# Layer 2's window attention: from one tile after another to a loop of slots in fixed order

## The chip, the cores and the metric

The program runs on one core of one Trainium2 chip. Its time is the device time of one execution in microseconds (us), and lower is better. The core has five engines that work side by side and meet at semaphores: TensorE (PE; weight loads are listed as PEld), VectorE (DVE), ScalarE (ACT), GpSimd (POOL) and SyncE (SP), which here only issues transfers. All data is 32-bit float.

## What is computed

Four layers run over two images of 1024 tokens with 256 channels. Layers 0 and 1 are global attentions; layer 2 is a window attention and a mixture of experts; layer 3 is an additive attention and a second mixture of experts. The change is inside layer 2, between the end of layer 1 and the first expert. In the reference, cut to what matters (the roll by half a window is done beforehand, by the way x is loaded):

```python
# t: (2, 1024, 256); H = 8 heads of D = 32; windows of 64 tokens
u = ln(t)                                          # over the 256 channels
q, k, v = (u @ w_qkv.T + b_qkv) by head
sim = (q . k) * D ** -0.5 + rel_pos[head, i - j]   # inside each window
sim = where(mask, -inf, sim)                       # last window of an image
out = softmax(sim) @ v                             # per head, heads joined
t = t + out @ w_out.T + b_out
# experts: route every token to two of 8
probs = softmax(ln(t) @ Wr + br);  top two, weights normalised to sum 1
t = t + sum over the two of weight * (gelu(xn @ W1[e] + b1[e]) @ W2[e] + b2[e])
```

The experts' own layer norm has a gain and a bias for each expert, so a routed token is normalised twice.

## The kernel before

**Tiles.** The tokens are 16 tiles of 128 (NT = 16), 8 to an image (IT = 8), two windows to a tile. `t` holds tokens on partitions, `uT` channels on partitions in two chunks of 128 (CC = 2). `CH` is 512 tokens, four tiles.

**Norm and turn.** After layer 1, `run` turns the stream into `t` (L846 to L851). `layer_norm` then normalises all 16 tiles (statistics L100, a square root on ScalarE L89, L104), and `to_channels` turns them into `uT` (L115 to L120). The small loads of the later layers (`Late.__init__`, such as L929's input `sb_wa`) go out on SP's queue at the same time.

**Window attention.** `scores(i)` projects q and k for four tiles at a time (L734, L740, L742), then v for its tile (L752, L756; a column of ones is appended to each head by L749), takes the scores of both windows (L767), scales them and adds the relative bias (L772), subtracts the row maximum (L778, L779), and writes the exponentials, not yet normalised, into the block diagonal of a 128x128 matrix per head (L782). `values(i)` turns these eight matrices on TensorE (L790, copied out by L791 on ScalarE and VectorE), multiplies each with its head's values (L795; the ones column yields the row sums), normalises the result (L797, L799), turns it into channels (L803, L805), projects it (L808), adds the bias (L812), and adds it into `t` on GpSimd (L813). The loop emits `scores(i + 1)` ahead of `values(i)`.

**Routing.** When tile 7, the last of image 0, has been emitted, `after` runs all of `dispatch(2, 0)` at once: `norm` and `channels` for the image (L956 to L974), the router (L1040), some 60 small VectorE operations that rank the experts and give each token two slots (L1044 to L1136), with a count over the tokens on TensorE in their middle (L1072), a second norm, 16 indirect transfers that scatter the tokens to their slots in memory (L1006, on GpSimd's queue), and 8 steps that add the experts' output bias (L1015 to L1021).

**Order.** In all of layer 2 a planner in the framework sets the order on each engine: an instruction that it holds to be ready goes first by its place in the program's text, and one of later text fills a gap. So an engine may draw later work ahead. Only where a `manual_schedule` stands do the engines named in it keep the order of the text. After the attention, `Late.run` merges the rest by a plan: each entry names a generator, what must be issued ahead of it, start and end on a common scale, and a number of pieces. E20 (experts of image 0) runs from 0 to 185, D21 (routing of image 1) from 5 to 165. For an expert tile the tokens are loaded from the slots (`xr`, L1168), the two weight matrices are gathered by an indirect transfer (`ew`, L1158), and the products are L1201 and L1215.

## Time and profile before

| What | us |
|---|---|
| Median of the runs shown (3204.81 to 3214.53) | 3204.91 |
| Profiled execution | 3201.66 |
| Its span | 3200.0 |
| Norm and turn, then first projection (L734) | 1789 to 1813.5 |
| Window attention, image 0 | 1813.5 to 1911 |
| Routing of image 0 | 1911 to 1960 |
| Window attention, image 1 | 1960 to 2033 |
| First load of expert inputs (L1168) | 2033.46 |
| Experts of image 0 | to 2234 |

The profile was taken in one execution, and every instruction in it has a start and a duration on its engine. A group such as "L790 x128" is one line of the kernel with all its executions. The view of busy time by stretch sums each engine's work between two marks and gives the clock that TensorE was granted, 1.00 being full speed. The chain of work follows, back from an end, what released each step. "Idle before, releaser" is how long an engine stood before an instruction and what it stood for. An average over the whole program says little here, since the stages have different limits; the stretches from 1789 to 2234 us are the ones to read.

### The profile page before, as it was taken

Reading aid. Unit: us, or ns where it says so; the run is one execution under the profiler, and the core shown is the slowest. Engines: PE = TensorE matmul, PEld = TensorE weight load, DVE = VectorE, ACT = ScalarE, POOL = GpSimd, SP = SyncE. Lnnn points to the kernel's source line nnn. Section 1 sums busy time; section 2 is a strip of 40 time slices with the busy share of each in tenths; the row PEclk is TensorE's granted clock in tenths of the full one; section 3 lists DMA queues with packets and bytes.
Section 4 is the critical chain, followed back from the end, with each engine's and each line's share of the span. In section 5 each row is a group of like instructions: output and inputs, shape, how many; then the busy total and the mean of one; then the engine's idle time right before and its main releaser. Section 6 shows DMA issues by size and latency. Waiting matters only on the chain.

```text
span 3200.0 us, 71583 instructions
## 1 busy us (share of the span) xinstructions
PE 2927.8 (91%) x29446; PEld 1895.9 (59%) x29446; DVE 1877.1 (59%) x3723; ACT 1998.1 (62%) x2980; POOL 403.5 (13%) x558
## 2 busy tenths in 40 slices
PE   7999999999999998999999787899899898997937
PEld 4565566656666656566667454798566432663726
DVE  5998898989898987355345454543422323233333
ACT  1887788888788886466466221211588887777801
POOL 3000000000000000000000002233211202224223
PEclk9999999999999999899999786899999998998968
DMA  3000000000000000000000100488554201554526
GB/s 120 3 3 3 3 3 3 3 3 3 3 3 3 3 3 16 13 1 2 1 1 2 25 1 27 176 317 309 196 196 176 75 1 65 168 161 130 180 78 226
DMA packets 179894, 216.08 MB, mean 68 GB/s; under 512 B 118816, under 2 KB 147120, under 8 KB 167792
## 3 DMA queue, kind: packets, MB, share of 16 engines
q0 software_dynamic: 36864, 175.17, 16.0%
q1 hardware_dynamic: 141264, 35.87, 5.0%
q8 instruction: 232, 3.80, 0.5%
q14 instruction: 94, 0.77, 0.1%
q10 hardware_dynamic: 1440, 0.47, 0.1%
HBM read 181.24 MB, written 29.49 MB: 66 GB/s over the span
## 4 chain that ended last, share of the span: by engine, by line
PE 84%; DVE 4%; DMA 4%; issue 4%; POOL 2%; ACT 1%; SPq 0%; POOLq 0%; ACTq 0%; DVEq 0%
PE ps_o L358 15%; PE ps_s L282 15%; PE ps_h L1201 8%; PE ps_y L1215 7%; PE ps_e L1351 7%; PE ps_t L340 5%; PE ps_s L153 4%; PE ps_o L220 4%; PE ps_t L183 4%; PE ps_v L1388 2%; PE ps_t L642 2%; DMA slots_in<-u,rt_slot 2%; PE ps_av L795 1%; PE ps_out L537 1%; PE ps_mm L734 1%
## 5 line engine op out<-in xcount | busy, mean ns | idle before, releaser
L319 ACT ACTIVATE sc<-sc,sa_shift 128x1024 f32<-128x1024 f32 x512 | 585.1, 1148 | 51.1 <-DMA sa_shift<-sa_min 50.9
L1342 ACT ACTIVATE th<-kT,qb 128x1024 f32<-128x1024 f32 x512 | 541.4, 1134 | 99.7 <-PE ps_e L1351 90.0
L282 PE MATMUL ps_s<-kT,qT 64*32 64x512 f32 x8192 | 503.8, 596 | 9.3 <-ACT sc L292 8.7
L358 PE MATMUL ps_o<-wt,v 128*64 128x128 f32 x6144 | 503.6, 276 | 0.0
L358 PEld LDWEIGHTS ps_o<-wt,v 128*64 128x64 f32 x6144 | 442.4, 137 | 42.6 <-issue 42.6
L332 DVE STREAM_TRANSPOSE wt<-sc 128x768 f32<-128x768 f32 x512 | 465.7, 943 | 0.4 <-ACT sc L319 0.4
L292 ACT COPY sc<-ps_s 128x1024 f32<-128x1024 f32 x256 | 257.5, 1006 | 118.4 <-PE ps_s L282 43.4
L1201 PEld LDWEIGHTS ps_h<-xe,ew 128*128 128x128 f32 x2320 | 284.5, 198 | 60.2 <-issue 38.2
L1201 PE MATMUL ps_h<-xe,ew 128*128 128x128 f32 x2320 | 298.8, 284 | 14.6 <-DMA ew<-in_l_up,rt_rows 8.4
L303 DVE TENSOR_REDUCE sa_least<-sc 128x1 f32<-128x1024 f32 x256 | 306.1, 1196 | 1.6 <-ACT sc L292 1.5
L289 DVE TENSOR_SCALAR_CACHE_REDUCE sc<-ps_s 128x1024 f32<-128x1024 f32 x256 | 301.4, 1177 | 6.1 <-PE ps_s L282 6.1
L1351 PE MATMUL ps_e<-th,pick 128*32 128x512 f32 x2048 | 297.9, 621 | 3.2 <-DVE sc_a L1358 2.9
L1215 PE MATMUL ps_y<-ew,h 128*128 128x256 f32 x1160 | 274.4, 385 | 8.9 <-ACT h L1190 7.3
L159 DVE TENSOR_SCALAR_CACHE_REDUCE sc<-ps_s 128x1024 f32<-128x1024 f32 x128 | 151.8, 1222 | 179.2 <-PE ps_s L153 179.1
L1215 PEld LDWEIGHTS ps_y<-ew,h 128*128 128x128 f32 x1160 | 213.1, 191 | 68.0 <-issue 19.3
L358 PE MATMUL ps_o<-wl,v_odd 128*64 128x128 f32 x2048 | 252.3, 277 | 0.0
L282 PEld LDWEIGHTS ps_s<-kT,qT 64*32 64x32 f32 x8192 | 126.6, 106 | 200.4 <-issue 170.6
L1190 ACT ACTIVATE h<-hb 128x512 f32<-128x512 f32 x145 | 90.4, 624 | 246.0 <-DVE hb L1206 232.6
L1206 DVE TENSOR_TENSOR hb<-ps_h,ew 128x512 f32<-128x512 f32 x145 | 100.2, 691 | 236.7 <-PE ps_h L1201 210.4
L340 PEld LDWEIGHTS ps_t<-ident,sc 128*128 128x128 f32 x1024 | 107.5, 141 | 216.2 <-issue 167.8
L358 PEld LDWEIGHTS ps_o<-wl,v_odd 128*64 128x64 f32 x2048 | 221.5, 137 | 0.0
L340 PE MATMUL ps_t<-ident,sc 128*128 128x128 f32 x1024 | 168.5, 287 | 4.6 <-ACT wl L341 3.9
(272 smaller groups left out, 3579.5 us busy)
## 6 DMA issues: line engine op xcount, KB each, us to landing
xr<-slots_in SPq DMA_DIRECT2D x99, 128.0 KB, 3.2
slots_out<-y SPq DMA_DIRECT2D x99, 128.0 KB, 3.5
sa_got<-sa_least SPq DMA_DIRECT2D x512, 0.5 KB, 1.8
sa_shift<-sa_min SPq DMA_DIRECT2D x512, 0.2 KB, 1.7
slots_in<-zero POOLq DMA_DIRECT2D x46, 128.0 KB, 2.2
sa_sums<-sa_total SPq DMA_DIRECT2D x256, 1.0 KB, 1.8
xT<-in_x SPq DMA_DIRECT2D x4, 496.0 KB, 5.1
ew<-in_l_up,rt_rows POOLq DMA_INDIRECT x99, 5.7
```

The source lines that it names most:

```text
L282: nc.tensor.matmul(ps[r][S * c : S * (c + 1), a, :].rearrange("p (b i) -> p b i", i=S), lhsT=qT[half, p, S * i : S * (i + 1)], rhs=keys[ha ...
L289: nc.vector.tensor_scalar(scores[m][0], flat[0], 1.0, None, ALU.mult, ALU.min, accum_out=least[m // 2][:, 0, h : h + 1])
L292: nc.scalar.copy(scores[m][1], flat[1])
L303: nc.vector.tensor_reduce(least[m // 2][:, 1, h : h + 1], scores[m][1], AX.X, ALU.min)
L319: nc.scalar.activation(scores[m][r], scores[m][r], AF.Exp, bias=shift[m // 2][:, r : r + 1], scale=-1.0, accum_out=total[i][:, 2 * p + r, ...
L332: nc.vector.transpose(weights[i, h][:, 2 * p + r, :], scores[m][r][:, :DIRECT])
L340: nc.tensor.transpose(ps[:, g, r, :], s[:, at : at + P], self.ident)
L358: nc.tensor.matmul(sums[i][64 * k : 64 * (k + 1)], lhsT=values, rhs=w, start=(h == 0 and j == 0 and t == 0), stop=(h == 1 and j == 1 and t ...
L1201: nc.tensor.matmul(ps[:, j, :], lhsT=a[:, c, at : at + P], rhs=x[:, c, :], start=(c == 0), stop=(c == CC - 1),)
L1215: nc.tensor.matmul(ps, lhsT=h[:, j, :], rhs=w2[:, j, :], start=(j == 0), stop=(j == HB - 1))
L1342: nc.scalar.activation(h, keys, AF.Tanh, bias=self.qb[b][:, s // G, g : g + 1])
L1351: nc.tensor.matmul(pe[i][c * U : (c + 1) * U, a, :], lhsT=self.pick[:, k, :], rhs=h[:, a, :], start=(k == 0), stop=(k == G - 1),)
```

## The change

The attention becomes a loop of 20 slots whose order on TensorE and ScalarE is that of the text. A tile passes through five stages in five slots: value and scores in slot i, turn in i + 2, sums in i + 3, output in i + 4. The projections are taken in quarters, four slots ahead. The weights are normalised before they are turned: VectorE takes the row sum and its reciprocal, and GpSimd multiplies the exponentials by it while it writes them into the block diagonal (a ring of three). Both halves of the turned weights are copied by ScalarE. The sums have the values as TensorE's stationary operand and the turned weights as the moving one, so that the result has channels on partitions, and the second turn goes. The ones column goes too.

The norm and the turn are done for each image: image 0 ahead of the loop, image 1 in slots 0 to 5. They use `Late.norm`, whose inverse root is computed with VectorE operations alone. The routing of image 0 enters the loop from slot 10, three steps to a slot, and what is left of it goes into the plan as D20. The functions `layer_norm` and `to_channels` are removed.

```diff
@@ -684,7 +656,10 @@
-    def window_attention(self, t, u, uT, after):
+    def window_attention(self, t, late):
+
+
+
         tc, nc = self.tc, self.nc
@@ -694,6 +669,7 @@
             sb = ctx.enter_context(tc.tile_pool(name="wa_sb", bufs=2))
             psum = lambda name, bufs: ctx.enter_context(tc.tile_pool(name=name, bufs=bufs, space=PSUM))
             p_mm, p_s, p_av = psum("wa_mm", 3), psum("wa_s", 1), psum("wa_av", 1)
+            late.misc = lambda shape, name: p_mm.tile(shape, F32, name=name, tag="ps_mm")
             w_qkv = self.load(w, "w_qkv", "(c p) o -> p c o", p=P)
             w_out = self.load(w, "wa_w_out", "(c p) o -> p c o", p=P)
@@ -719,45 +695,47 @@
             nc.vector.memset(last[WIN + SHIFT : P, :, 0:SHIFT], MASKED)
-            probs = [w.tile([P, H, P], F32, name=f"probs{i}") for i in range(2)]
...
+            RING = 3
+            probs = [w.tile([P, H, P], F32, name=f"probs{i}") for i in range(RING)]
+            for x in probs:
+                nc.gpsimd.memset(x, 0.0)
+
+            uT, q, k, v, pT, o = {}, {}, {}, {}, {}, {}
+
+            def normed(b):
+
+                u = w.tile([P, IT, C], F32, name="u")
+                uT[b] = w.tile([P, CC, N], F32, name=f"uT{b}")
+                yield from late.norm(lambda i: u[:, i, :], lambda i: t[:, b * IT + i, :], range(IT))
+                for half in range(2):
                     for c in range(CC):
...
-                v[i] = sb.tile([P, H, D + 1], F32, name="va", bufs=3)
-                nc.gpsimd.memset(v[i][:, :, D : D + 1], 1.0)
...
+                        ps = late.misc([P, 4, P], "ps_tr")
+                        for j in range(4):
+                            nc.tensor.transpose(ps[:, j, :], u[:, 4 * half + j, c * P : (c + 1) * P], self.ident)
+                        to = uT[b][:, c, half * CH : (half + 1) * CH].rearrange("p (k t) -> p k t", t=P)
+                        (nc.scalar.copy if c else nc.vector.tensor_copy)(to, ps)
+                        yield
+
+            def project(g, part):
+
+                if part == 0:
+                    q[g], k[g] = (sb.tile([P, CC, CH], F32, name=n) for n in ("qh", "kh"))
+                x, at = uT[g // 2], g % 2 * CH
+                ps = late.misc([P, CH], "ps_qk")
                 for c in range(CC):
                     nc.tensor.matmul(
...
+                        ps, lhsT=w_qkv[:, c, part * P : (part + 1) * P], rhs=x[:, c, at : at + CH],
                         start=(c == 0), stop=(c == CC - 1),
                     )
...
+                to = (q if part < CC else k)[g][:, part % CC, :]
+                if part < CC:
+                    nc.scalar.activation(to, ps, AF.Identity, bias=b_qk[:, part : part + 1])
+                else:
+                    nc.vector.tensor_scalar(to, ps, b_qk[:, part : part + 1], None, ALU.add)
+
+            def scores(i):
+
+                g, at = i // 4, (i % 4) * P
                 s = p_s.tile([P, 4, CH], F32, name="ps_s")
                 for o in range(CC):
                     for h in range(4):
@@ -768,56 +746,94 @@
                                 s[WIN * r : WIN * (r + 1), h, WIN * o : WIN * (o + 1)],
                                 lhsT=q[g][rows, o, cols], rhs=k[g][rows, o, cols], start=True, stop=True,
                             )
...
+                l = sb.tile([P, H, WIN], F32, name="l", bufs=3)
                 nc.vector.scalar_tensor_tensor(
                     l.rearrange("p (h o) k -> p h (o k)", o=CC), s[:, :, : CC * WIN], float(D) ** -0.5,
...
+                    (last if (i + 1) % IT == 0 else bias).rearrange("p (h o) k -> p h (o k)", o=CC),
                     ALU.mult, ALU.add,
                 )
...
+                m, rec = (self.small.tile([P, H], F32, name=f"wa_{n}") for n in ("m", "rec"))
                 nc.vector.tensor_reduce(m, l, AX.X, ALU.max)
                 nc.vector.tensor_tensor(l, l, broadcast(m, [P, H, WIN]), ALU.subtract)
+                nc.scalar.activation(l, l, AF.Exp)
+                nc.vector.tensor_reduce(m, l, AX.X, ALU.add)
+                nc.vector.reciprocal(rec, m)
                 for r in range(2):
                     rows = slice(WIN * r, WIN * (r + 1))
-                    nc.scalar.activation(probs[i % 2][rows, :, rows], l[rows], AF.Exp)
...
-                    nc.tensor.matmul(av[:, of, :], lhsT=ptT[:, h, :], rhs=v[i][:, of, :], start=True, stop=True)
...
+                    nc.gpsimd.tensor_tensor(
+                        probs[i % RING][rows, :, rows], l[rows], broadcast(rec[rows], [WIN, H, WIN]), ALU.mult
+                    )
+
+            def value(i):
+                x = uT[i // IT][:, :, i % IT * P : (i % IT + 1) * P]
+                v[i] = sb.tile([P, C], F32, name="va", bufs=4)
+                ps = late.misc([P, C], "ps_va")
                 for c in range(CC):
                     nc.tensor.matmul(
...
+                        ps, lhsT=x[:, c, :], rhs=w_qkv[:, c, 2 * C :], start=(c == 0), stop=(c == CC - 1)
+                    )
+                nc.vector.tensor_tensor(v[i], ps, b_v, ALU.add)
+
+            def turn(i):
+                pT[i] = sb.tile([P, H, P], F32, name="ptT")
+                for half in range(2):
+                    ps = late.misc([P, H // 2, P], "ps_pt")
+                    for h in range(H // 2):
+                        nc.tensor.transpose(ps[:, h, :], probs[i % RING][:, H // 2 * half + h, :], self.ident)
+                    nc.scalar.copy(pT[i][:, H // 2 * half : H // 2 * (half + 1)], ps)
+
+            def sums(i):
+
+                ps, x, y = p_av.tile([P, CC, P], F32, name="ps_av"), pT.pop(i), v.pop(i)
+                for o in range(CC):
+                    for h in range(4):
+                        at = D * (4 * o + h)
+                        nc.tensor.matmul(
+                            ps[D * h : D * (h + 1), o, :], lhsT=y[:, at : at + D], rhs=x[:, CC * h + o, :],
+                            start=True, stop=True,
+                        )
+                to_o(i, ps)
+
+            def to_o(i, ps):
+                o[i] = sb.tile([P, CC, P], F32, name="oT")
+                nc.scalar.copy(o[i], ps)
+
+            def output(i):
+                x = o.pop(i)
+                ps = late.misc([P, C], "ps_wo")
+                for c in range(CC):
+                    nc.tensor.matmul(
+                        ps, lhsT=x[:, c, :], rhs=w_out[:, c, :], start=(c == 0), stop=(c == CC - 1)
                     )
                 y = sb.tile([P, C], F32, name="y")
                 nc.vector.tensor_tensor(y, ps, b_out, ALU.add)
                 nc.gpsimd.tensor_tensor(t[:, i, :], t[:, i, :], y, ALU.add)
-            scores(0)
...
-                values(i)
...
+            for _ in normed(0):
+                pass
+            route, other = late.dispatch(2, 0), normed(1)
+            engines = mybir.EngineType
+            with tc.manual_schedule(engines={engines.PE, engines.Activation}):
+                for part in range(2 * CC):
+                    project(0, part)
+                for i in range(NT + 4):
+                    if i < NT:
+                        value(i)
+                        scores(i)
+                    if 2 <= i < NT + 2:
+                        turn(i - 2)
+                    if i + 4 < NT:
+                        project(i // 4 + 1, i % 4)
+                    if i < 6:
+                        next(other, None)
+                    if 3 <= i < NT + 3:
+                        sums(i - 3)
+                    if 4 <= i:
+                        output(i - 4)
+                    if i >= 10:
+                        for _ in range(3):
+                            next(route, None)
+            return route
@@ -851,21 +867,7 @@
                             nc.vector.tensor_copy(to, ps)
             late = Late(ctx, self, t)
...
-                self.layer_norm(u, t, 1e-5)
...
-                    self.to_channels(uT, u, psum)
...
-            late.run()
+            late.run(self.window_attention(t, late))
 class Late:
@@ -1412,7 +1414,7 @@
-    def run(self):
+    def run(self, route):
         psum = lambda name, bufs: self.ctx.enter_context(self.tc.tile_pool(name=name, bufs=bufs, space=PSUM))
         p_m = psum("lt_m", 2)
         self.sb = self.ctx.enter_context(self.tc.tile_pool(name="late_sb", bufs=2))
@@ -1420,7 +1422,8 @@
         self.p_x, self.p_h, self.p_y, self.p_e = psum("lt_x", 1), psum("lt_h", 2), psum("lt_y", 1), psum("lt_e", 1)
         plan = {
-            "E20": (self.experts(2, 0), (), 0, 185, 72),
+            "D20": (route, (), -12, 0, 24),
+            "E20": (self.experts(2, 0), ("D20",), 0, 185, 72),
             "D21": (self.dispatch(2, 1), (), 5, 165, 48),
             "C20": (self.collect(2, 0), ("E20",), 186, 225, 20),
             "E21": (self.experts(2, 1), ("D21",), 186, 440, 72),
@@ -1439,7 +1442,7 @@
         }
         self.issued = set()
         at = {name: start for name, (_, _, start, _, _) in plan.items()}
-        now = 0
+        now = min(at.values())
         def merge(until):
             nonlocal now
```

## The prediction

> **What bounds the kernel now.** First the whole chain of work that ended last: TensorE holds 84% of it, so time is won only where that chain holds something else, or TensorE work that can go. Then the busy time by stretch, cut at the marks of layer 2: norms (1789 to 1813 us), window attention of image 0 (to 1911), its routing (to 1960), attention of image 1 (to 2033), the start of the experts, the experts of image 0.
>
> ```profile
> PE 84%; DVE 4%; DMA 4%; issue 4%; POOL 2%; ACT 1%; SPq 0%; POOLq 0%; ACTq 0%; DVEq 0%
> ...
> 1813.00:1911.00 98.00, 82.49 (x668) 58.25 (x669) 48.85 (x117) 25.39 (x43) 6.35 (x15) 0.85 0.00 1
> 1911.00:1960.00 49.00, 25.08 (x117) 16.30 (x116) 30.96 (x141) 0.91 (x3) 7.66 (x8) 0.53 0.05 17
> 1960.00:2033.00 73.00, 60.70 (x415) 46.53 (x415) 33.39 (x92) 16.57 (x30) 15.11 (x23) 0.85 0.05 19
> 2033.00:2040.00 7.00, 3.54 (x15) 2.10 (x13) 5.72 (x22) 0.00 (x0) 5.23 (x6) 0.50 0.74 256
> 2040.00:2234.00 194.00, 191.77 (x1284) 176.73 (x1284) 82.20 (x236) 34.27 (x52) 60.74 (x63) 0.98 0.87 319
> ```
>
> Columns: stretch, length, busy PE, PE weight loads, DVE, ACT, POOL, granted clock, DMA share, GB/s. The experts fill TensorE at clock 0.98; the attention takes 98/8 = 12.3 us a tile with no engine full, and the routing takes 49 us with TensorE half busy at clock 0.53. Next, the chain through one tile, in order of time:
>
> ```profile
> 1977.98 0.45 PE ps_pt L790 x4
> 1978.43 0.03 ACTq L791
> 1978.46 0.04 issue
> 1978.50 0.59 ACT ptT L791
> 1979.09 0.14 issue
> 1979.23 1.96 PE ps_av L795 x16
> 1981.18 0.02 issue
> 1981.21 0.22 DVE wa_rec L797
> 1981.43 0.02 issue
> 1981.45 0.44 DVE o L799
> 1981.89 0.14 issue
> 1982.02 0.42 PE ps_mm L803 x2
> ```
>
> Weights are turned, copied, summed, normalised, turned again and projected, each waiting for the last: a chain of latencies inside a tile. Last, GpSimd's order of time, with the scatter of tokens to expert slots:
>
> ```profile
> 1951.00 0.97 POOL L1006 DMA_INDIRECT slots_in<-u,rt_slot  x1 [1.70 <-DMA slots_in<-u,rt_slot]
> 1953.68 0.97 POOL L1006 DMA_INDIRECT slots_in<-u,rt_slot  x1 [1.72 <-DMA slots_in<-u,rt_slot]
> ```
>
> Each of the 16 scatters waits until the one before has landed: 2.67 us each, 42.7 us in a row. They start at 1942.3 and the last is issued at 1990.9; now the second image's attention hides them.
>
> **The slot, part by part** (warm durations from the timeline). TensorE: value 4 matmuls, 0.86; scores 32 in 0.49 (L767); turn 8 in 1.04 (L790); one quarter of a projection, 6.87/4 = 1.72 (L734, slots 0 to 11); output 0.9. *Removed:* 16 sums with 128-column weights, 1.96, and the turn of o, 0.42, with the waits between. *Added:* 16 sums with 32-column weights and 128 moving columns; no row has this form. The nearest is layer 1's L220 (64 columns, 128 moving), 32 in 1.97, so 16 take 1.0. The Trainium skill ("TensorE: Matmul & The Clock Gate", LDWEIGHTS) prices a load at its columns over 1.2 ns: 27 ns, 16 in 0.43. I take 1.0; the bounds move a slot by 0.6, 16 slots by 9 us. Sum: 0.86 + 0.49 + 1.04 + 1.72 + 1.0 + 0.9 = **6.0 us**, without projection 4.3.
>
> ScalarE: one Exp of 128x512 in place of two of 64x512 (0.63 each), two copies at 0.585 (one was DVE's), oT 0.37, half a q at 0.69: 2.5. Its fixed order puts exp(i) ahead of the copies of turn(i-2); exp(i) starts 0.6 + 3 x 0.7 = 2.7 after scores(i) (as 1902.97 to 1906.30 shows with one copy between), so the copies end some 5.4 into the slot. Bank reuse then holds output to about 5: hidden under the 6.0 with projection; without it a slot is 4.8.
>
> DVE: value 0.42, scale and bias 0.69, max 0.69, subtract 0.68, sum 0.69, reciprocal 0.21, y 0.42, half a k at 0.75: 4.2, below 6.0.
>
> GpSimd: two multiplies of 64x512 and the add into t. The row is L813, 128x256 in 0.728, DVE's like add L812 0.425. Twice the elements per partition: at most 1.46, so 2 x 1.46 + 0.73 = 3.65. The skill ("GPSIMD Engine Reference", Engine selection) speaks against this: two-input elementwise work is about twice as slow there, and the section 1 table has its port contended by DVE instructions with two SBUF inputs. Its 2.6 cycles an element at 1.2 GHz give 1.11 each, 2.95 a slot. Beside DVE's subtract, L813 once took 1.11 instead of 0.73 (1879.29): all stretched so, 5.5. All three stay below 6.0, and the turn comes two slots later, so row and rule give the same slot; I take 3.65. Queued behind a multiply are the adds into t and the scatters; the memset of the ones column (L749), on which the queue now stands for TensorE, is gone. SP's queue has nothing behind the expert input loads that is due earlier.
>
> **The sum, in profile time.** Norm of one image only: half of 16 normalisations (0.33 apart) and of the 8.9 us of turns saves 2.7 + 4.4, less a little: projections start at 1807, not 1813.5. The sqrt on ScalarE becomes 12 small DVE operations of 0.2, covered by DVE's wait for the sb_wa load until 1802.6, which stays. Without the cover, 2.4 us. First projections 8.9: **1816**. Slots 0 to 3: two of 3.1, then 6.5 each, since turn(0) waits for the Exp table (1.28) and the new chain sum, reciprocal, multiplies: 19, **1835**. Slots 4 and 5 with the other image's turns, 7.2 each; 6 to 9 at 6.0: **1873.5**.
>
> Routing of image 0 enters as three steps a slot from slot 10. All it issues counts. Slot 10, turns, 7.4. Slot 11 ends in a stall: output(7), y 0.42, GpSimd add up to 1.4, statistics 0.6, inverse root 2.4, four normalisations 1.4, with DVE queueing some 7 us with TensorE standing, since its order is fixed: 13.5. Slot 12, 4.8 and the router's 32 matmuls (4.4 warm, L1040): 9.2. Slot 13 waits for 15 DVE operations of 0.26 amid the slot's own: 9. **1912.5**. From the counts to the first scatter it is now 5 us with DVE free; here DVE also owes 4.2 a slot and 9.7 for the second norm: 12. First scatter **1925**. Attention itself ends near 1939 (two slots of 6, a drain of 13).
>
> So the end of the stage moves to the scatters. The D20 leftovers (7 scatters, 8 bias steps at 1.92 each, L1019) go to the late plan; the bias steps (15 us) hide beside the scatters and the scatters do not. 16 x 2.67 = 42.7 bare; now 48.6 from first to last issue with other POOL work between, plus 2.4 to land. I take 48: the first expert input is loaded at **1973**, now 2033.46: **60.5 saved**. Expert weights can be fetched meanwhile, but up to six 1 MB loads slow scatters: image 1's, under such load, are 81 us from first to last.
>
> **The experts of image 0** (2033 to 2234): 23 tiles at 7.24 (spacing of the input loads), TensorE-full. In it stand 13.5 us of image 1's routing: turns 1.0, router 4.4, counts 0.7, bias 8 x 0.9. With TensorE idle from 1939 to 1973 the planner may draw these ahead: 0 to 13.5; I take 9, and 3 for weights that are there already (first up-matmul now 6.5 after the load). **12**. All later work keeps its order.
>
> Sum: 60.5 + 12 = 72.5; span 3200.0 to 3127.5, the profiled time 3201.66 to 3129.2. The median of the runs, 3204.91, lies 3.2 above the profiled one: **3132 us**.
>
> **Rivals.** (a) *Scatters earlier, gap filled:* sums at 0.43, no stall at slot 11 because the planner draws norms ahead (it did: L956 of tile 0 at 1841.8), first scatter 1912, all 13.5 drawn ahead: 3132 - 13 - 5 = 3114. For: DVE gaps. Against: DVE owes about 61 us in slots 10 to 16. (b) *Fixed order stretches the slots:* TensorE stands for DVE or GpSimd at 8 us a slot in place of 6 (28 us over 14 slots): 3160. For: in-order ScalarE with exp ahead of copies. (c) *Slower:* GpSimd becomes the bound, if half-height multiplies with a broadcast cost far more than their row. It decides from slots of 6 + 72.5/14 = 11.2 us, where 2m + 0.73 = 11.2, m = 5.2 us a multiply. At 6 us, 12.7 a slot: 3132 + 14 x 6.7 = 3226. Against: L813. (d) *Nothing won:* experts start no sooner because scatters crawl beside weight loads at 5.1 us each from the first: 1925 + 82 = 2007, still 26 saved: 3166 with the 12.
>
> **Chances.** Likeliest 0.58, (a) 0.17, (b) 0.13, (d) 0.05, (c) 0.05, no change 0.02. A difference under 0.3% (10 us) is what a measurement of this kernel can't tell from none. Range 3106 to 3162: (a) with a few us of better luck, up to (b); outside it (c), (d) and the tail. Faster 0.93, same 0.02, slower 0.05.
>
> **What would show it.** Right: slots 6 to 9 near 6 us with TensorE full; GpSimd's multiplies 1.1 to 1.5; no L797, L799, L803; a stall before image 0's second turns; the first xr load just behind the sixteenth scatter with attention over 30 us earlier; image 1's router ahead of the first up-matmul. Wrong: scores or turns waiting for GpSimd, weight loads between scatters stretching them to 5 us, or an xr load that does not wait for scatters.

## The result, and the profile after

The changed kernel takes 3158.78 us (median; 3157.64 to 3160.96) against 3204.86 for the kernel before, a ratio of 0.9849 with a 95% interval of 0.9836 to 0.9863. The forecast was 3132 us with a range of 3106 to 3162. So the sign and the range held, and the size did not: the profiled span went from 3200.0 to 3156.0, 44.0 us, where the sum said 72.5.

The chain of work that ended last, by engine, in the changed kernel:

```profile
PE 83%; DVE 6%; issue 3%; DMA 3%; POOL 2%; ACT 1%; SPq 0%; another core or an unknown queue 0%; POOLq 0%; ACTq 0%; DVEq 0%
```

VectorE has gone from 4% to 6% of it, the transfers from 4% to 3%. Busy time by stretch (columns as before), cut at the marks of the changed kernel: norm, slots 0 to 5, slots 6 to 9, slot 10 to the end of the attention, two stretches up to the first expert, experts of image 0.

```profile
1790.00:1814.00 24.00, 14.29 (x56) 8.71 (x57) 21.02 (x92) 5.43 (x12) 3.11 (x11) 0.79 0.35 79
1814.00:1851.00 37.00, 31.07 (x344) 18.66 (x343) 26.12 (x45) 11.83 (x23) 12.07 (x12) 0.95 0.01 1
1851.00:1882.00 31.00, 25.12 (x274) 15.80 (x273) 23.98 (x62) 8.00 (x18) 10.28 (x12) 0.94 0.00 1
1882.00:1956.00 74.00, 53.25 (x529) 37.33 (x527) 59.60 (x200) 15.42 (x34) 28.18 (x30) 0.82 0.03 10
1956.00:1994.00 38.00, 20.50 (x75) 12.48 (x75) 28.98 (x138) 0.26 (x1) 15.08 (x17) 0.57 0.55 194
1994.00:2007.00 13.00, 10.14 (x24) 4.41 (x25) 6.00 (x24) 0.00 (x0) 7.16 (x8) 0.50 0.37 121
2007.00:2184.00 177.00, 176.66 (x1220) 165.60 (x1220) 59.50 (x123) 31.44 (x49) 54.15 (x58) 0.99 0.91 317
```

In slots 6 to 9 VectorE (third pair) is almost as busy as TensorE, and from slot 10 to 1994 us it is the busiest engine. Two stretches, 51 us, still run at a clock of 0.50 to 0.57 before the experts fill TensorE. A good part of the missing gain lies there.

**The slots.** The value matmul (L772) opens a slot. Slots 6 to 9 take 6.6, 7.5, 7.7 and 9.1 us, not 6.0. The chain of waits there, in order of time:

```profile
1857.80 1.03 POOL probs L763
...
1860.03 0.74 POOL t L810
1860.79 0.44 DVE n_st L958
...
1861.44 0.59 DVE l L750
1862.05 0.70 DVE wa_m L756
1862.77 0.70 DVE l L757
1863.51 0.04 issue
1863.56 0.64 ACT l L758
1864.22 0.70 DVE wa_m L759
...
1865.31 1.04 POOL probs L763
```

TensorE isn't in it. The planner has drawn the statistics of image 0's routing norm (L958) ahead, one tile to a slot, as VectorE isn't one of the engines in fixed order. L958 of tile i-4 waits for the add into `t` on GpSimd (L810), which is queued behind the two multiplies of slot i (L763); those wait for slot i's softmax on VectorE; and the softmax of slot i+1 (L750 onwards) is queued behind L958. The circle closes at 7.51 us (1857.80 to 1865.31).

**The scatters.** GpSimd's order of time, last column the idle time and what ended it:

```profile
1980.35 0.99 POOL L1008 DMA_INDIRECT slots_in<-u,rt_slot  x1 [3.31 <-DMA slots_in<-u,rt_slot]
1983.95 0.97 POOL L1008 DMA_INDIRECT slots_in<-u,rt_slot  x1 [2.61 <-DMA slots_in<-u,rt_slot]
1992.39 1.03 POOL L1008 DMA_INDIRECT slots_in<-u,rt_slot  x1 [7.47 <-DVE rt_lg L1103]
1993.73 0.97 POOL L1008 DMA_INDIRECT slots_in<-u,rt_slot  x1 [0.30 <-issue]
```

Image 0's scatters start at 1937.45 and the first expert input is loaded at 2002.12, 64.7 us later. Six weight loads stand among them (from 1955.26 to 1980.35 the scatters are 4.2 us apart in the mean, in the kernel before 2.67), and the scatter at 1992.39 is image 1's first one: it waits 7.47 us for its own routing while image 0's last three stand behind it. This looked like the loss. It was not the only one, as the next view says: TensorE just ahead of the experts.

```profile
1994.39 0.37 PE L1017 MATMUL ps_wT<-ident,rt_p 128*8 128x128 f32 x1 [7.11 <-DVE rt_p L1134]
1995.65 1.22 PE L1021 MATMUL ps_b<-sb_l_b,wT 8*128 8x256 f32 x2 [0.89 <-DVE wT L1019]
...
2004.65 0.63 PE L1178 MATMUL ps_x<-ident,xr 128*128 128x128 f32 x2
2005.25 1.22 PE L1021 MATMUL ps_b<-sb_l_b,wT 8*128 8x256 f32 x2
2006.40 0.38 PE L1017 MATMUL ps_wT<-ident,rt_p 128*8 128x128 f32 x1
2006.57 1.06 PE L1203 MATMUL ps_h<-xe,ew 128*128 128x128 f32 x4
```

The first up-matmul (L1203) follows without a gap on the bias steps (L1017, L1021) of *image 1*, which begin when image 1's routing has run through VectorE. The expert input is turned (L1178) 1.9 us before. In e8 below, where no bias step stands between that turn and L1203, L1203 starts 3.4 us after the load; by that, an estimate, it could have started here at 2005.6. So the input and the bias steps come due within about 1 us of each other: as long as the bias steps stay ahead of L1203, an earlier input alone wins nothing.

### The profile page after: what moved, and what is told of

The parts are those of the page before. It is cut to its first block, busy times and chain, and to the rows that moved or that the text cites. A ratio compares the mean times of both kernels' runs of the same rounds, so it can differ in the third digit from the quotient of the medians.

```text
span 3156.0 us, 71520 instructions
## 1 busy us (share of the span) xinstructions
PE 2890.6 (92%) x29414; PEld 1853.4 (59%) x29414; DVE 1882.7 (60%) x3729; ACT 1988.0 (63%) x2975; POOL 435.6 (14%) x575
## 3 DMA queue, kind: packets, MB, share of 16 engines
q0 software_dynamic: 36864, 175.17, 16.5%
## 4 chain that ended last, share of the span: by engine, by line
PE 83%; DVE 6%; issue 3%; DMA 3%; POOL 2%; ACT 1%; SPq 0%; another core or an unknown queue 0%; POOLq 0%; ACTq 0%; DVEq 0%
PE ps_o L330 15%; PE ps_s L254 15%; PE ps_h L1203 8%; PE ps_y L1217 8%; PE ps_e L1353 7%; PE ps_t L312 5%; PE ps_s L125 4%; PE ps_o L192 4%; PE ps_t L155 4%; PE ps_v L1390 2%; PE ps_t L614 2%; DMA slots_in<-u,rt_slot 1%; PE ps_out L509 1%; PE ps_qk L443 1%; POOL got L1263 1%
## 5 line engine op out<-in xcount | busy, mean ns | idle before, releaser
L1203 PEld LDWEIGHTS ps_h<-xe,ew 128*128 128x128 f32 x2320 | 281.9, 196 | 52.5 <-issue 30.4
L1203 PE MATMUL ps_h<-xe,ew 128*128 128x128 f32 x2320 | 295.3, 282 | 7.2 <-DVE xe L1182 3.8
L341 POOL TENSOR_TENSOR diag<-ident,sa_rec 32x128 f32<-32x128 f32 x64 | 24.9, 389 | 1171.9 <-DVE sa_rec L338 1171.9
```

The source lines that it names most:

```text
L1203: nc.tensor.matmul(ps[:, j, :], lhsT=a[:, c, at : at + P], rhs=x[:, c, :], start=(c == 0), stop=(c == CC - 1),)
```

## The experiments

Runs are compared by the time since the first value matmul of the same execution, because the layers before reach it between 1811.5 and 1816.9 us in these runs. "Attention ends" is the start of the last add into `t`; "first up" is L1203, "first gather" the end of image 0's experts.

| Kernel | median us | ratio to before [95%] | slot 10 | first scatter | attention ends | first up | first gather |
|---|---|---|---|---|---|---|---|
| changed kernel | 3158.78 | 0.9849 [0.9836, 0.9863] | 68.2 | 123.1 | 142.0 | 192.3 | 369.5 |
| e1_add_vector | 3151.77 | 0.9832 [0.9811, 0.9852] | 63.3 | 119.7 | 133.2 | 188.7 | 365.8 |
| e2_hold_stats | 3152.25 | 0.9833 [0.9816, 0.9849] | 60.4 | 119.8 | 138.7 | 189.3 | 367.5 |
| e3_scatter_order | 3156.40 | 0.9852 [0.9832, 0.9872] | 66.9 | 123.0 | 141.8 | 192.4 | 370.8 |
| e4_scatter_weights | 3155.81 | 0.9847 [0.9823, 0.9871] | 67.0 | 123.1 | 141.9 | 181.8 | 370.0 |
| e5_experts_first | 3152.46 | 0.9831 [0.9805, 0.9858] | 66.9 | 123.0 | 143.9 | 182.6 | 367.2 |
| e6_all | 3140.36 | 0.9802 [0.9776, 0.9828] | 63.3 | 119.7 | 132.7 | 175.3 | 360.0 |
| e7_vector_multiply | 3151.11 | 0.9832 [0.9807, 0.9857] | 63.9 | 121.4 | 138.7 | 187.8 | 366.2 |
| e8_planner_order | 3146.49 | 0.9817 [0.9793, 0.9842] | 63.6 | 122.9 | 130.1 | 187.5 | 367.1 |
| e9_route_after | 3172.07 | 0.9905 [0.9888, 0.9921] | 68.2 | 141.4 | 118.8 | 206.8 | 383.2 |
| e10_planner_all | 3131.71 | 0.9777 [0.9761, 0.9794] | 56.5 | 109.6 | 116.9 | 163.0 | 348.8 |
| e11_vector_all | 3147.10 | 0.9824 [0.9807, 0.9840] | 63.9 | 121.6 | 138.7 | 178.0 | 362.2 |
| e12_bias_scalar | 3135.41 | 0.9776 [0.9761, 0.9792] | 57.1 | 112.0 | 119.5 | 164.7 | 350.4 |

All intervals but those of e6, e9, e10 and e12 overlap that of the changed kernel, so the marks inside the executions carry the reading, not the medians. The marks have a spread too, since each is read from one execution: up to slot 10 e3, e4 and e5 do the same work as the changed kernel and reach it at 66.9 to 67.0 us, the changed kernel at 68.2. The difference lies in slots 2 and 3, which no edit touched.

### Does the circle set the slots? (e1, e2)

First way to open it: the add off GpSimd's queue.

```diff
-                nc.gpsimd.tensor_tensor(t[:, i, :], t[:, i, :], y, ALU.add)
+                nc.vector.tensor_tensor(t[:, i, :], t[:, i, :], y, ALU.add)
```

> The add of the attention's output into t (L810) on VectorE instead of GpSimd; nothing else is edited. Theory A (closed loop): slots 6 to 9 take 7.7 us because the statistics L958 of the routing norm, drawn ahead between two slots on VectorE, wait for the add into t on GpSimd, which stands behind the slot's two multiplies L763. On VectorE the add no longer stands behind them: slots 6 to 9 fall to 6.0 to 6.5 us (the value matmul L772 of slot 10 starts near 1877 in place of 1882.5), the first scatter L1008 comes near 1930 in place of 1937.45, and the time is 3149 to 3154 us (after: 3158.8). Rival B (VectorE itself is slowed while GpSimd multiplies, or has too much to do): VectorE gets 0.42 us a slot more, the slots stay at 7.7 to 8.1 us and the time is 3158 to 3166 us.

Second way: leave the add, and hold the statistics. `issue_after(x)` queues the instructions that its block emits for x's engine behind x; it sets an order only.

```diff
-                nc.vector.reciprocal(rec, m)
+                made = nc.vector.reciprocal(rec, m)
+                if i == 9:
+                    late.hold = made.ins
...
-        for k, i in enumerate(tiles):
-            nc.vector.bn_stats(st[:, k, :], src(i))
-            nc.vector.bn_aggr(mv[:, k, :], st[:, k, :])
+        with self.tc.issue_after(self.hold) if self.hold else ExitStack():
+            for k, i in enumerate(tiles):
+                nc.vector.bn_stats(st[:, k, :], src(i))
+                nc.vector.bn_aggr(mv[:, k, :], st[:, k, :])
```

> The statistics L958/L959 of image 0's routing norm are queued on VectorE behind the reciprocal L760 of slot 9; the add into t stays on GpSimd. Theory A (closed loop): slots 6 to 9 fall from 7.7 to about 6.1 us, as in slots before the statistics are drawn ahead; the statistics of four tiles (4 x 0.6 us) then stand in slot 10, which grows by up to 2.4 us. Net 3 to 5 us: time 3153 to 3156 us. Rival B (GpSimd's multiplies slow VectorE, whatever stands on it): slots 6 to 9 stay above 7.3 us, slot 10 grows, time 3159 to 3163 us.

In e1 slots 6 to 9 take 6.3, 6.3, 6.5 and 8.6 us, together 3.2 us less than in the changed kernel. Slot 10 starts at 1876.55 and the first scatter comes 3.4 us earlier after the first value matmul. In e2 TensorE's order of time (the edit moves L772 to L773 and L963 to L964) reads:

```profile
1853.50 1.03 PE L773 MATMUL ps_va<-sb_w_qkv,uT 128*128 128x256 f32 x4
...
1859.49 1.03 PE L773 MATMUL ps_va<-sb_w_qkv,uT 128*128 128x256 f32 x4
...
1877.26 1.03 PE L773 MATMUL ps_va<-sb_w_qkv,uT 128*128 128x256 f32 x4
...
1887.88 2.21 PE L974 MATMUL ps_tr<-ident,u 128*128 128x128 f32 x8 [3.91 <-DVE u L964]
...
1903.74 2.21 PE L974 MATMUL ps_tr<-ident,u 128*128 128x128 f32 x8 [6.61 <-DVE u L964]
```

Slots 6 to 9 end at 1859.49, 1865.42, 1871.34 and 1877.26, 5.9 to 6.0 us each, with GpSimd's multiplies still beside them. So the work drawn ahead, and not the multiplies' effect on VectorE, held those slots: in slots 6 to 8 as the circle, which e1 opens as well, but not in slot 9. That slot stays at 8.6 us in e1, since the planner has also drawn four normalisations of the routing (L963) and statistics of its second norm into VectorE's queue there. But the statistics now come due in slots 10 and 11, which take 12.6 and 15.9 us in place of 8.6 and 15.2: slot 10 starts 7.8 us earlier, the first scatter only 3.3. The work drawn ahead was not waste; it was paid in the wrong place.

### Do the scatters set the start of the experts? (e3, e4, e5)

```diff
+                with self.tc.issue_after(self.sent[2, 0].ins) if key == (2, 1) else ExitStack():
-                nc.gpsimd.indirect_dma_start(
+                    self.sent[key] = nc.gpsimd.indirect_dma_start(
...
```

> Image 1's scatters are queued on GpSimd behind the last scatter of image 0; nothing else is edited. Theory C (order of the queue): the first scatter of image 1 stands 7.47 us for its routing with the last three of image 0 behind it, which then alternate with image 1's. Without it the 14th to 16th scatter follow at 2.67 us, the first expert input is loaded near 1994 in place of 2002.1, and the time is 3149 to 3153 us. Rival D (the start of the experts is not set by the last scatter, or what image 1's scatters lose comes back later): the load moves and the time stays within 3156 to 3162 us.

and with it, for the expert weights:

```diff
+            with self.tc.issue_after(self.sent[2, 0].ins) if key == (2, 0) and m < 3 else ExitStack():
-            nc.gpsimd.indirect_dma_start(
+                nc.gpsimd.indirect_dma_start(
                     out=w[:, :width], out_offset=None, in_=packed[k],
...
```

> As e3_scatter_order, and the first five expert weight fetches of image 0 (L1160) are also queued behind its last scatter. Theory E (weight loads slow the scatters from 2.67 to 3.6 us each beside them): the last eight scatters win 7 us more, the first expert input is loaded near 1987; but the first weights then land some 6 us after the last scatter, so that the first up-matmul (2006.8 in after) comes near 1993 to 1996, and the time is 3145 to 3150 us. Rival F (weights become what the first tiles wait for: five loads of 1 MB in a row at 4 to 6 us each): the first tiles wait and the time is that of e3_scatter_order or up to 6 us above it.

In e3 the first expert input is loaded 7.8 us earlier after the first value matmul (180.0 against 187.8), as expected, and the first up-matmul comes no earlier (192.4 against 192.3), again straight behind the last bias step of image 1. Rival D holds. In e4 the load comes 16.5 us earlier and the first up-matmul 10.5 us earlier, and the experts end no sooner, because now the bias steps run among them. TensorE's order of time in e4:

```profile
1993.52 0.80 PE L1203 MATMUL ps_h<-xe,ew 128*128 128x128 f32 x2 [0.64 <-DVE xe L1182]
...
2117.12 0.69 PE L1022 MATMUL ps_b<-sb_l_b,wT 8*128 8x256 f32 x2
...
2119.95 0.27 PE L1018 MATMUL ps_wT<-ident,rt_p 128*8 128x128 f32 x1
```

A bias step costs 0.96 us of TensorE there at full clock (0.69 + 0.27), eight of them 7.7 us at most. The stretch from first up to first gather grew from 177.2 to 188.2 us, so most of what the start gained went into work that the changed kernel had done in the gap. Of the other 3.3 us, waits of 1.37 (a weight load) and 0.61 us (VectorE) are 2.0. The time is that of e3, as rival F had it, but the late weights are little of the cause; the gain went where neither theory had put it. The scatters themselves now take what the forecast gave them: 48.2 us from the first one to the load, in e3 57.0, in the changed kernel 64.7.

So an earlier start pays only if it removes more idle time than the work that it pushes into the experts. e5 also moves image 1's routing behind the experts' first steps, on both engines, and keeps tile 0's weights early:

```diff
-            with self.tc.issue_after(self.sent[2, 0].ins) if key == (2, 0) and m < 3 else ExitStack():
+            with self.tc.issue_after(self.sent[2, 0].ins) if key == (2, 0) and 0 < m < 3 else ExitStack():
...
-            nc.tensor.transpose(ps, p[:, i, :], self.ident)
+            with self.tc.issue_after(self.first["up"]) if key == (2, 1) else ExitStack():
+                nc.tensor.transpose(ps, p[:, i, :], self.ident)
...
-            nc.vector.tensor_copy(to, ps)
+            with self.tc.issue_after(self.first["xe"]) if key == (2, 1) else ExitStack():
+                nc.vector.tensor_copy(to, ps)
```

> As e3_scatter_order, with the weight fetches of tiles 1 and 2 behind the last scatter of image 0 (those of tile 0 stay early), and image 1's routing held on VectorE, from its counts on (L1075), behind the first xe (L1182) of image 0's experts, and its bias steps (L1017) on TensorE behind the first group of up-matmuls. Theory G (what starts the experts in after is not the last scatter but image 1's routing and bias steps, which stand ahead of the first up-matmul; from there TensorE is full to the end, so that only idle or half-clock time before it can be won): the first up-matmul comes 15 to 19 us earlier than in after, the stretch from it to the first gather of L1263 grows from 177 to 190 to 193 us (eight bias steps at 0.96, one cold start, the counts), and the time is 3151 to 3156 us, ratio to before 0.983 to 0.9845. Rival H (weights or inputs become what the first tiles wait for): the stretch grows by as much as the start moved or more, time 3158 to 3164 us.

The time is where theory G put it, its terms are smaller: the start moved by 9.7 us, not 15 to 19 (tile 0's two weight loads slowed the scatters again; the load is at 176.2, in e4 at 171.3), and the stretch grew by 7.4 us, not 13 or more. The first gather comes 2.3 us earlier.

Together with e1:

> e5_experts_first together with e1_add_vector (the add into t on VectorE). Theories A and G: both gains add, as they lie in different stretches (attention slots; start of the experts): 6 to 7 us below e5_experts_first, 3144 to 3149 us, ratio 0.981 to 0.9825. Rival: the later attention was cover for the scatters, so that only one of the two counts: 3150 to 3154 us.

3140.36 us, some 4 us below the expectation. Up to the first gather the gain is 9.4 us where the two alone give 3.7 + 2.3; a further 6.4 us come after it, in work that no edit touched (below). That the two give more together than alone fits the view before the experiments, where input and bias steps came due together; in e6 TensorE waits 12.55 us for the expert input.

### Undoing one part at a time (e7, e8, e9)

The multiplies on VectorE:

```diff
-                    nc.gpsimd.tensor_tensor(
+                    nc.vector.tensor_tensor(
                         probs[i % RING][rows, :, rows], l[rows], broadcast(rec[rows], [WIN, H, WIN]), ALU.mult
```

> One part undone: the two multiplies of weights by reciprocals (L763) on VectorE in place of GpSimd; order, placement and all else as in after. By the row of L757 (two inputs from SBUF, 512 a partition, 0.69 us) VectorE gets 1.4 us a slot. Theory A: the closed loop is gone (the add into t stands behind nothing on GpSimd), slots 6 to 9 take 6.3 to 7.0 us; in slots 10 to 15, where VectorE is 80% busy, the 1.4 us come on top: 6 x 1.4 = 8; net 3160 to 3166 us. Rival B (GpSimd's multiplies cost VectorE as much as they relieve it, since L757 stretches from 0.69 to 1.5 us beside them): 3150 to 3157 us.

It is faster than the changed kernel, 3151.11 us, where theory A had it slower; rival B's number is right. The circle is open: slots 6 to 9 take 6.6, 6.9, 7.3 and 7.4 us. And VectorE does not pay the price that I worked out, 1.4 us a slot: slots 10 to 14 take 54.3 us, in the changed kernel 53.7. The 32 multiplies are 23.3 us on VectorE (0.73 each), but its busy time from 30 us ahead of the first value matmul to the first gather rises only from 226.8 to 237.6. The subtraction (L757) in the changed kernel, and then in e7 (duration in ns: least, median, most):

```profile
L757 DVE TENSOR_TENSOR l<-l,wa_m x16: 668/692/1536, 1817.3 to 1941.6; 128x512 f32<-128x512 f32 x16
```

```profile
L757 DVE TENSOR_TENSOR l<-l,wa_m x16: 658/691/692, 1817.6 to 1938.6; 128x512 f32<-128x512 f32 x16
```

Summed over their records, VectorE's other instructions in that stretch take 9.6 us less in e7, so GpSimd's help costs VectorE some 40% of what it relieves. Only 1.7 us of it lie in L757, two of whose sixteen are long in the changed kernel; 3.7 lie in the normalisations L963, the rest mostly in single small operations of the routing that run beside a multiply. With e5's order added:

> e5_experts_first with the multiplies L763 on VectorE (e7_vector_multiply) and the add into t on GpSimd as in after: the other way to break the closed loop. Theory A: either way breaks it, so the gain is near that of e6_all: 3143 to 3148 us. Rival B (the multiplies beside VectorE's own two-input work are the larger loss, 1.5 in place of 0.69 us): below e6_all, 3134 to 3139 us.

3147.10 us, as theory A said. By the marks e6_all is 2.2 us earlier at the first gather (360.0 against 362.2), so the two ways to open the circle are close; that the multiplies are better left on GpSimd is not shown beyond that.

The order of TensorE and ScalarE left to the planner:

```diff
-            with tc.manual_schedule(engines={engines.PE, engines.Activation}):
+            with ExitStack():
                 for part in range(2 * CC):
```

> One part undone: the order of TensorE and ScalarE inside layer 2's attention is left to the planner; the new mathematics, the split by image and the routing's place in the text stay. Theory: the fixed order of slots is what hides the chain within a tile (scores, Exp, multiply, turn, sums); left to the planner, slots 6 to 9 take 8 us or more, and the time is 3170 to 3190 us. Rival: the fixed order costs as much as it gives (TensorE stands 6.0 us in slot 11 and 6.6 in slot 13 for routing work that it meets in a fixed place): slots 11 and 13 lose their stalls, and the time is 3145 to 3157 us.

3146.49 us, the rival's time. Slots 6 to 9 are no faster in sum (31.2 us, in the changed kernel 31.0), and slot 11 still stands (21.7 us). But the attention ends 11.9 us earlier, since scores of later tiles are drawn ahead into the stall (the lines below show it for e10); image 1's routing starts earlier by that, its bias steps end about when the expert input arrives, and the first up-matmul comes 4.8 us earlier. So the fixed order, which the change was about, gained nothing in this kernel. What it cost is less sure than the medians say: up to the first gather e8 wins 2.4 us, and 6.9 us more lie behind it, in work that no edit touched. The first scatter is no earlier (122.9 against 123.1).

The routing of image 0 behind the attention, as before:

```diff
-                    if i >= 10:
-                        for _ in range(3):
-                            next(route, None)
```

> One part undone: image 0's routing is no longer traced inside slots 10 to 19 of the attention but behind it, with the late plan, as in before; mathematics, fixed order and the split by image stay. Theory (the interleaving is what the gain comes from): slots 12 to 15 fall from 9.9, 13.2 and 6.7 us to 5 us each and the attention ends near 1925 in place of 1956; the routing then runs alone, 31 us from the end of the attention to the first scatter as in before, less 5 us of statistics drawn ahead: first scatter near 1950 in place of 1937.45, time 3167 to 3174 us. Rival (VectorE, 80% busy in slots 10 to 15, has the same work in both places and sets the end in both): first scatter 1935 to 1942, time 3153 to 3162 us.

3172.07 us, as the theory said: the attention ends at 118.8 instead of 142.0, the first scatter comes at 141.4 instead of 123.1. Interleaving the routing is worth 13.7 us at the first gather (383.2 against 369.5). No run undoes the new arithmetic or the split of the norm by image, so their shares are not measured. The interleaving isn't what slows slots 6 to 9: slots 7 to 9 take 7.5, 7.7 and 9.1 us here too, because the planner draws the statistics ahead wherever the text has them.

### The best combination (e10, e12)

> e6_all with the order of TensorE and ScalarE in the attention left to the planner (e8_planner_order). Theory: the planner's order won 2.4 us up to the first gather and 3 us behind it in e8_planner_order; the first lies in slots 10 to 15, which e6_all doesn't touch, so that it adds: 3135 to 3139 us. Rival: both win the same stall (statistics and normalisations in front of TensorE in slots 10 to 13): 3139 to 3144 us.

3131.71 us, ratio 0.9777, faster than both kernels, and below both expectations (3135 at the least): the two gains more than add. The planner's order brought the first scatter 0.2 us forward in e8, and 10.1 us here (109.6 against 119.7 in e6). Why it does so only with the add on VectorE is not shown. Busy time by stretch, slots 0 to 9, 10 to 19, up to the experts, experts:

```profile
1814.00:1871.00 57.00, 52.84 (x619) 33.44 (x618) 52.30 (x106) 20.68 (x40) 18.98 (x18) 1.00 0.01 2
1871.00:1940.00 69.00, 51.00 (x541) 35.94 (x539) 63.06 (x238) 16.26 (x34) 22.60 (x21) 0.86 0.09 29
1940.00:1979.00 39.00, 18.10 (x66) 13.38 (x65) 18.07 (x83) 0.26 (x1) 14.56 (x15) 0.50 0.35 128
1979.00:2163.00 184.00, 183.66 (x1232) 169.41 (x1233) 70.48 (x181) 31.56 (x49) 59.60 (x62) 0.98 0.90 320
```

and TensorE's order of time, first in slot 11, then at the start of the experts:

```profile
1886.99 0.49 PE L745 MATMUL ps_s<-kh,qh 32*64 32x64 f32 x32 [2.03 <-DVE l L750]
1889.11 0.49 PE L745 MATMUL ps_s<-kh,qh 32*64 32x64 f32 x32 [1.63 <-DVE l L750]
1892.94 0.74 PE L745 MATMUL ps_s<-kh,qh 32*64 32x64 f32 x32 [3.33 <-DVE l L750]
...
1976.16 0.66 PE L1178 MATMUL ps_x<-ident,xr 128*128 128x128 f32 x2 [11.21 <-DMA xr<-slots_in]
1977.39 0.79 PE L1203 MATMUL ps_h<-xe,ew 128*128 128x128 f32 x2 [0.56 <-DVE xe L1182]
```

The planner sends the scores of three later tiles into the stall in which the fixed order stood. With the routing of image 1 held back, TensorE waits 11.21 us for the expert input behind the scatters, as it does in e5 (4.37 us), e6 (12.55) and e11 (8.02): in these runs the scatters are what the forecast took them for, the thing that sets the start.

VectorE is 91% busy in the second stretch (63.06 of 69), so I expected to gain by relieving it:

```diff
-            b_v, b_out = self.load_row(w, "b_v"), self.load_row(w, "wa_b_out")
+            b_v, b_out = self.load(w, "b_v", "(c p) -> p c", p=P), self.load_row(w, "wa_b_out")
...
-                nc.vector.tensor_tensor(v[i], ps, b_v, ALU.add)
+                nc.scalar.copy(v[i], ps)
...
-                nc.scalar.copy(o[i], ps)
+                for c in range(CC):
+                    nc.scalar.activation(o[i][:, c, :], ps[:, c, :], AF.Identity, bias=b_v[:, c : c + 1])
```

> e10_planner_all, and the bias of the values is no longer added on VectorE (L775, 0.42 us a slot): since the weights of a token sum to one, it is added per channel by ScalarE where it copies the sums (L799, two activations of 128x128 in place of one copy of 128x256), and the values are copied by ScalarE. VectorE is relieved of 0.42 us a slot, ScalarE, under 25% busy in slots 10 to 15, gets some 0.6 us more. Theory (VectorE, 80% busy in slots 10 to 15, sets them): these slots get 0.4 to 0.8 us shorter each, the first scatter comes 3 to 6 us earlier against the first value matmul, the time is 3126 to 3129 us, ratio to before 0.9755 to 0.9768. Rival (waits between engines set these slots, not VectorE's load; ScalarE's copies add to the chain): 3130 to 3134 us.

3135.41 us, ratio 0.9776 beside 0.9777: nothing gained, and the first scatter comes 2.4 us later (112.0 against 109.6), though VectorE's busy time in the second stretch (now 1869 to 1938) is 59.52 us in place of 63.06 and ScalarE's 20.67 in place of 16.26. The theory as I had it falls: less work for VectorE did not shorten these slots. What does, the ScalarE copies in the chain or the single scores buffer that TensorE waits for above, stays open. The edit also gave ScalarE more to do, so it is no test of VectorE's load alone.

## Why the prediction was right or wrong

The sign and the order of events were right. That the time lies inside the range is in part luck: the first scatter and the scatters behind it cost 29.2 us more than forecast, the experts gave 7.1 back, and the upper end, 3162, was drawn for a rival whose reason holds only in part.

- **Norm and start of the loop:** right. The first projection starts at 1807.2 (1807 predicted), the first value matmul at 1814.3 (1816), slot 4 at 1836.5 (1835). Slots 0 to 3 took 22.2 us in place of 19; the earlier start made up for part of it.
- **Slots 6 to 9 at 6.0 us:** the working was right and the slot was not: 7.7 us in the mean. e2 shows 5.9 us once nothing is drawn ahead. The step that failed is "all three stay below 6.0": I added busy time per engine and did not follow the queues. I had named the add into `t` as queued behind a multiply, had seen in the profile before that the planner draws norms ahead, and did not join the two. Cost: 7 us up to slot 10 (1882.5 in place of 1875.3, by e2's pace); less than half of it is the circle (3.2 us, by e1), most of the rest the normalisations drawn into slot 9.
- **Multiply and sums:** the row gave 1.46 us for a multiply, the Trainium skill ("GPSIMD Engine Reference", 3.1) an estimate of 1.11; measured 1.04. For the 16 sums the row gave 1.0, the rule ("TensorE: Matmul & The Clock Gate", LDWEIGHTS) an estimate of 0.43; measured 0.64. Neither moved the slot much: without the work drawn ahead it took 5.9 us in e2. The port contention that the skill names showed, but in the changed kernel mostly on VectorE's side: two subtractions took 1.52 and 1.54 us in place of 0.69, while GpSimd's multiplies took 1.03 to 1.19.
- **Slots 10 to 13:** predicted 7.4, 13.5, 9.2, 9.0; measured 8.6, 15.2, 9.9, 13.2. The two stalls are where they were put (5.98 us for L963, 6.59 us for L1067). From the end of slot 13 to the first scatter it takes 8.0 us, where I had put 12. First scatter 1937.45 for 1925: 9.0 us of the 12.5 were lost by slot 10, 3.5 behind it.
- **Scatters, 48 us, and with them the experts' start at 1973:** wrong twice. They take 64.7 us, since the sum put nothing for the weight loads and image 1's scatters that come between them, though I had named the weight loads. e3 takes out image 1's scatters (57.0 us), e4 the weight loads too (48.2 us). And they were not alone in setting the start. The step "with TensorE idle from 1939 to 1973 the planner may draw these ahead: 0 to 13.5" counted image 1's routing as filler. It filled the gap past its end: bias steps at half clock, 1.92 us each (1995.65 to 1997.57), stood ahead of the first up-matmul. e3 shows that faster scatters alone win nothing, e5 that the start moves by 9.7 us when the routing is held back too.
- **Experts, 12 us saved:** too small. From the first up-matmul to the first gather 17.1 us went (194.2 to 177.2), where I had put 9, and 2.1 between load and first up-matmul (3): 19.1 from the load. TensorE's busy time in this stretch fell from 192.0 to 176.9 us, more than all the routing that I had counted (13.5; its terms add up to 13.3), and its idle time from 2.2 to 0.3. This is the other side of the late start, not a separate gain; e4 gives most of it back.
- **"All later work keeps its order":** the order held, the time did not. From the first gather to the end VectorE, ScalarE and GpSimd run the same 879, 658 and 242 instructions in the same order as before, and take 972.2 us, before 965.8. TensorE is busy for 825.9 us of it, before 818.6, at a mean granted clock of 0.90, before 0.91. 2.5 us of the 6.4 lie between the first gather and the first tanh. The experiments with this order (all but e9) take 965.3 to 970.8. I put nothing for such a shift; what causes it stays open.

The sum, re-done with measured terms: 72.5 - 12.5 (first scatter) - 16.7 (scatters) + 7.1 (experts, measured from the input load) - 6.4 (after) = 44.0.

Of the rivals, (b) named the right family, TensorE standing for VectorE and GpSimd, and 3160 us; but it had 8 us in all fourteen slots, by the fixed order and ScalarE's place in it. e8 takes the fixed order away and leaves slots 6 to 9 as long as they were; what it won back lay at the end of the attention. Rival (d)'s time was near too, but its mechanism, scatters crawling beside weight loads, is not what set the time alone: e3 and e4 sped them up and won nothing.

## What to carry to other kernels

Adding up each engine's work in a loop gives its pace only if no chain runs through several queues and back. Wherever one engine's order is left to a planner, look for work that it can draw into the loop and ask what that work waits for and what stands behind it. When a stage is shortened, ask what else was waiting for the same moment: here the second image's routing took over the start of the experts, so two causes had to be removed together. Work that fills a gap at half clock ahead of a full stretch is not free once the gap closes; compare what it costs in either place.

## What the hardware showed unexpectedly

- A VectorE subtraction with two inputs from SBUF (L757, 128x512) takes 0.69 us. One that starts while a GpSimd multiply (1.04 us) runs ends 0.55 us behind the multiply's end, wherever in it it starts: in the changed kernel 1.54 and 1.52 us (0.05 and 0.07 us into the multiply), in e10 1.19 and 0.95 (0.40 and 0.64 us into it). The other way round, two multiplies that start while a subtraction runs take 1.41 and 1.38 us in e10 (from 1890.85 and 1902.26). With no multiplies on GpSimd (e7) the longest of the 16 subtractions is 0.692.
- One bias pair of matmuls takes 1.22 us on TensorE in the gap (changed kernel, clock 0.50) and 0.69 inside the experts (e4, clock 1.00); a whole step takes 1.92 us in the gap, and 0.96 of TensorE time in the experts.
- Scatters of 128 rows follow each other at 2.67 us alone (e4, 1963.40 to 1966.07) and at 4.2 us in the mean with a 1 MB weight load queued between each two (changed kernel, 1955.26 to 1980.35, six intervals of 3.0 to 5.6).
